# Two FNO attention layers on one core: ones written by GpSimd and VectorE, loads by halves on two queues, the identity loaded first, and another order of the instructions

## The chip, the core and the metric

The kernel runs on one core of one Trainium2 chip. The metric is the device time of one execution in microseconds (us). A core has a matrix engine (TensorE, PE in the profile), three engines for elementwise work (VectorE, DVE; ScalarE, ACT; GpSimd, POOL), and SyncE (SP), which here only issues transfers. Transfers between DRAM and the on-chip memory can be issued by SP and by ACT; the profile calls their issuing queues SPq and ACTq. PE writes its results to PSUM, eight banks of 128 partitions x 2 KB; the other data lies in a memory of 128 partitions.

## The reference

Two layers of the same form are applied to x of shape (2, 56, 128, 128): batch, channels, height, width. Cut to what matters:

```python
xn = inorm(xa, g1, b1)                       # each channel by itself, (2*56, 1, 128, 128)
k, q, v = (fno_layer(xn, w, b, sw, sb) for K, Q, V)   # 8 heads each
scores = einsum('baks,bals->bakl', qh, kh) / 128      # channels against channels, per head
out = softmax(scores) @ vh
out = fno_layer(out, Pw, ...)                # heads back to one channel
att = inorm(out + xa, gan, ban)
an = inorm(att, g2, b2)
h = fno_layer(an, M0w, ..., norm=True, act=True)      # exact gelu
h = fno_layer(h, M1w, ..., norm=True)
y = inorm(h, gmo, bmo) + att
```

`fno_layer` is a spectral convolution (a 2-D real FFT of which 32 x 16 modes are kept, a complex product per mode, and the inverse) plus a 1x1 skip. All arithmetic is fp32.

## The kernel before, in words

The image of one batch lies in `X2` as 128 partitions: channels 0 to 55 at partitions 0 to 55 with one half of the rows (`c`=0), the same channels at partitions 64 to 119 with the other half (`c`=1). Partitions 56 to 63 and 120 to 127 hold ones; one of them serves as a bias row in later matmuls. A load of x (line 328) brings one half of 16 rows of `X2`: 56 partitions x 2 x 4 KB, 448 KB. Sixteen of them bring both batches.

A layer and batch go through these stages; the names are those of the functions:

- `turned` (L496): PE transposes eight rows of the image (16 transposes per unit), ACT or VectorE copies them out of PSUM into `P`, and statistics are taken (VectorE's bn_stats for layer 0, batch 0, otherwise ACT).
- `modes_chain` (L583): mean and variance become the scale `gv` (GpSimd, a power of -0.5, `root`, L313) and the shift `sh`. PE makes the modes of the image from `P`, then four pieces of `P` of 128x1792 are normalised in place (`affine`, L655, on ACT or VectorE).
- `gram` and `gram_chain` (L662, L675): channel-by-channel products over the normalised image.
- `scores`, `values`, `softmax_chain`, `mix_chain`, `heads`, `norms_chain` (L726 to L917): attention in mode space.
- `gelu` (L943): per eight rows the image is formed again (x or the stored result of layer 0 is loaded into one of the three buffers of `xr`, L953), gelu, transposes, and modes.
- `h_chain` and `end` (L1006, L1088): the last spectral part, and per eight rows the result, which goes to `store` (layer 0) or `out` (layer 1). Each is moved in two halves of 224 KB.

`prepare` (L357) makes the layer's weight tables: first 17 small operations on `sm` (GpSimd), then three products over `stage` (the loaded weights, L405 to L407), many small operations, and the tables `WU`, `WT`, `WM`.

Nothing is scheduled automatically. Every operation is recorded as a unit with the engines that could do it (`Work`, L183), and the string `ORDER` (L21) lists all 1410 units in the order of issue, each as the difference to the unit before and a letter for the engine: T for PE, V (and W, a second form) for VectorE, S for ACT, G for GpSimd, Q for SP, N for leaving an optional unit out. `PLACES` (L77) gives the PSUM bank of each result. An engine issues its units in this order and waits, at each, for the data and buffers that the unit needs; a transfer's issue waits in the same way. Since every instruction is issued by one helper, the profile gives L214 as the line of nearly all.

A PE operation uses a tile of the array, by the rows and columns of its weights rounded up to 32, 64 or 128. Two neighbours in PE's order can have different tile shapes; counted over the whole order before, 292 neighbours do.

The first units in the order before, by engine (a half of 16 rows is named by batch, its first eighth of the image g, and c):

- SP: x b0 g4 c0; constants of 416 columns (208 KB, the identity among them); x b0 g6 c0; sm; x b0 g2 c0; x b0 g0 c0; weights (544 KB); constants of 112 columns; then x of batch 1 (seven halves); constants of 768 and 708 columns; the ones (four transfers of 256 KB, two of them before the first loads of xr).
- ACT: x b0 g4 c1, g6 c1, g2 c1, g0 c1; the first copies; x b1 g2 c1.
- GpSimd: clears of xf and xr; the 17 small operations of `prepare`; the three products on `stage`; gv.

Of the kernel before, what the change touches and what calls it, by code (L numbers as in the profile page):

```python
# [14 lines left out]
B, K, N = 2, 56, 128  # L15
# [6 lines left out]
29G -1G -23Q 1S -6Q 52T 1V -46Q 4Q 43V -27G -19S -4S -1Q 82G -83S -1Q 48T 1S 1V -41Q -1Q 7S 39T 1S 32G -31V 32G  # L22
-31T 1V -13T 1S 13V -12V -5T 1S 1V -5T 1S 1V 48G -53T 1S 1V 87V 1T 1V 1G -114Q 55T 21V 40V -39V -57V -3V 35T 76T
-6T 3T -2V 8T -7T 2V 1T -71S 59V -62S -49Q -6Q 131V -124Q 49S 65V 2G 17S -6V -15T 1S 21V -72T 1S 1S -70Q 79T
-29T 22V 73T -59V 60T 1T -100T 36V -35S 3S 80T 3T -52V -24S 34T 56T -13V -132Q 77V -76Q 4Q 129S -56V -22T 1S 2T
1S 21T -32S 35G 54V 8T 1T -57V 49V 9T 2S -68V 10V -31S 32V -47S 103T -53T 55S -93S 94S -90T 1S 72S -44V -4V 7T
-90Q 81V 85T -162Q 145T -67V -22S -50V 74V 12V 18V 53V -31T -133Q 355Q -267V 140V -216V 157T 60T 1V 1G -225V -4Q
158G 2G 4T 1V -19V -1V -55V 284Q 1Q -280G 37S 15G 16T 68S 6T -3G -68T 72V -150V 1V 8G 149T -16V -62S 72T 1V
-145G 74T 62T -61V 68T -4G -141G 149T -95T 94T 11S 106Q -1Q -125S -247Q 173G -67T 260Q -203V -152Q 127V 45T 90T
-87T 1T 560G -548V 51V -52G -91S 151V -90G 1G 99S 478G -472T 1T 1T -76S -125G 194S -247V 239V -2T -65T 68T 1V  # L30
-99G 113T -7S 8T -77V 1T 77T 1T 3S -12T 1V -77V 69G -94G 111S -16S -62S -13T 1V -3T 8T 1V 104T -280G 168S 113S
-190V 187V -3V -183V 91T 62S -74T 13S 1T 1V 75S 2T -75T 77V 1G -94S 17T 1T 1T -4T 77S -72V 1V 100T -95V -4T 100S
-11T -87S 9V 79V -87T 104T -31G -71T 1V 102S -31G -65T 1V -6G 8V 5V 68T -74G 78T 1S -2T 4T 1S -88V 1T 1S -9V 15V
1T 1V 1V 134Q -52T 1S -29T 21T -20V -51T 1V 73T -76T 1V -72G 133G 450G -374T -61T 12V -7T 1S 50T -43S 44V 1N
-71G 20T 73Q -18S 2T -50V -161G 216S -215G 154V 69T 1V -67G 419G -415T 1S 49S 16Q -15S -86G 1G 101T -60T 1T 60V
-12T 1V 13T -61T 66S -73T 8T 61S 1S -69V 3T 42G -44T 1V 6S 1V -43G 83T -36T 1V 60T 5Q 339G -459G -119G 210S 5T
20S -23S 26Q 2T 1V -20N 22Q -17N 16N 18Q -90T 46V -41T 1V 1G 8V -14S 1S 73T -1Q 2S 1G -17T 1S -50V 84Q -6Q 2T 1V
-14T 1S -67T 1V 70S -17T 14S 16T -29V -59G 1T 5G 2V 1T 68T -131G 132S 8Q 3V 2T 1S -2N -88V 74S -3T 20S -83V 385V
-321V 22S -83T 2T 213Q -214V 65T 15T 1S -79V 69N 126Q -199G 194Q 6Q -4T 19Q -129T 109Q 2V 4T -158S 159V 1N -116S
-2S 3T 1V 115T -6N 23Q -222V 206S 4S 1S 7T -149V 22T 2S 130T -4V -127S 2T 2S 125Q 3V -127V 140Q 153G -290V -2V  # L40
287G -173T 1S 178G -296S 131T 1S -19T 184G -167N -16S -110T 2T 1V 1T 1V 127S -11N 22Q -13T -15T 16S 2S -127G 1V
1V 1G 1V 130T 4Q 1T 1S -7Q 2V 1N 22Q -48V -103T 1S 35S 98G -97G -39T 1V 136T 1S 1S -16T 1V -117T 1V 275T 1V 1V
-218S 83T -93N 68T 17S -16V 160V -138Q -4T 5Q 138V -132T -1Q -3S -6S -141G 6S 58V -57G 129T 1V 15S -151T 1V 52N
18N 70T 1V -99S 110T 1S -112T 12V -10G 1W -21N 134S -2T 1S 3T 1S -138T 12W 127T 1V -138N 30G -51T 22V 46N 20S
-65G -13N 141S -148W 8N 1V 42T 106T 2V -120N 13S 79S -77T 52S 52S 2T -107S 99S -86V -9W 106V -1S 2V 4V -139N 13T
1S 233T 1S -267G 22T 1S 133V -122S -43N 160V -94G -63T 66T 95T 2T 2T 1V 2V -1G 2V -115N 13S 211T -277S 278V 3V
-112G 1V 109V -223T 1S 118V -167T 21S -20S 162T 1V 102G -101T 1V 45N 61V -213S 171N -57N -46V 112N -229T 1S 39S
170S 1G -89G 38T 1V -3T 1V 23N 82T 1V -273S -9S 19S 217T 60V -88S 11N 28N 50T 1V 1G -61N 1V 65G -87T 12W 11G 61S
6T 3T -10V 13T -5V 1T 2V 1T -92V 96T -2V -114N -2T -17N 67V -59S 113T -72N 93S -6V -2T 3T -15V 21S -115G 1W 119T
-128V 82T -62G -187Q 285V 3S -79T 87T -140G 54S 1S 86T -107T -13N 3T -12V 119V 4V -76V 83T 1T -40V -296Q 47Q  # L50
181S -10S -209Q -1Q 38Q 190T 1S 103S -11V -147T 113G -110V -167Q 39Q 237G -19G 62T 1T 1T -301Q 156W 95V -103G 9N
-176Q 196Q 40T -36S 10S 113V -1S 232Q -338Q 21S 32V 35G -36V -30S 86T 1V 1V 1G -130Q 28Q 46V -82T 155T 1V -155S
82T -93T 12S -11S 182T -21T 1V -172T 193V -192S 367Q -180T 1V -16T -171S 365Q -279G 70T 19T 9T -10T 2V -302Q
-37Q 281G -243Q 172S 54V -92S 158G 67V 1T -78V -40G 119V -68G -81G 91T 59G 2S 3V -63V -2T -38T 27G -358Q 255Q
182T 1V -410Q 412T 1V -69T 1T -41V 98V -45V -328Q 151Q 176G 2S 1V -93G 83S 62T 3T 111Q -118V 8T 1V -198Q 52V 76T
1S 71T 7V -218Q 317Q -355Q 191T -8T 65T 14T 1T -71S 43T 4V -55S 9T 1S 56V 8S -60T 1T 1T 1T 58V -62T 60V -6T 13T
1T 1T -30V 16V 2V 1V 12T -108V 43S 1V 1T 2S 64S -2T 22T -85V -10T 65T 9T 3S -76V 12V 63V -56V 96T -8T -87T -9T
2T -54V 136S 18T -48S 43S -94V 7V -6G 1G 6G 1V 54T 2V -1S 36S -17T 19S -7T -81G -4V 74V -302Q 18Q 266G 30V -85T
-8T 83T -9G -65V -8V 9V 69T 3T -18T 1V 19V 2T 1S -47V -99G -1G 72T 1V 63G -1G 10T 3T 1T 12V -323Q 236T 1V -72G
2G 218Q -61S -8T 55T -5T -49S 5V 3V 1T 1S 45V 15T -20V 1N -40T 46T 5S -46T -164G 165T -295Q 290V -319Q 56Q 309S  # L60
6T -343Q 344S 8Q 1Q -3V -11T 1V -43T 57T 1V -57T 1S -5T 63T -100G 78N 21N 12Q -76T 66S -58V 5V 57S -11N -6T 44Q
-16Q -80V 53V -218G 173T 2S 9V -56G 46S 67Q 1T 1V -7T -60T 17V -15T 1V 1G 5T 1V 61T -1Q 2V -61G -60G 135Q -18N
-120G 113S 26T -32S 4S -3T 1S -52V 69T 18T -17S 4S -73T 1S 81V 2Q -78V 1V 76N -55S 39N 18Q 2V 1N 47Q -6Q -121T
1V 1V 79T -18T 19S 60Q -94T 38S -37V 13S 2V -60T 1V -73G 190Q -55T 56T -117T 1V 61S 1T 1V 54S -191G 195T -3G
-42S 43Q 3S -45T 31V -30S 3T 43T 1S 4S -47V 1T 1V -67S 42S 21S 47T 1V 8Q -208G 214T -2Q -14S 11T -52T 1S 55Q 2V
1N -21G 15V 7T -6N 11S 6Q -10S -16S -43V 44T 1V 46Q -21Q -409G 340T 4V -2S 1V -2V 5V -165G 229T 5T -67V 65Q 1Q
2S -71T 66V 1N -12T -15T 16S -2S -52T 2T 37V -36V 2V 66T 1S 4S -19T 1V 24Q 2T 1V -81G 2V 1G 80Q 2T -1Q 2S -31T
19T -1S -17V 19V 13T 5S -89V 66T 1V -64T 1S 79G -82T 1V 89T -19T 20V -7S -37S 39T 1S -78V -4T 67V 60S 34S -74T
1V 40G -126T -1V 83S -4S 9T 1S 1V 1T -89V 149T 3T -99G 39V 3V -39S 37V 82S -84S 6V 63N -1G 2N 1W 1N -13N 14Q
-74S 26S 49S -71T 23G 50S -71T 2T 17T -16V 2V 32S -7N -26G 2V 16N -15G 16N 1W 31N 2T 1S -50V 3T -2T 22N 1W 27N  # L70
1Q 10T 11N -48N 28Q -26Q 45G -68S 93N -17N 59N -25S -112V 15N 9Q 48N 1W -11G 1N -47Q 12G 46N 2S 27S -28Q -40N
29N 1W 55S -103S 49N 1Q 1Q -65G 1T 1V 3S 18T 3N 109N -108N 1W 82G -81N 1Q 3N -2S 45N -73T 1V 30T 1N 1V 1N 1Q 1S
69T 3N 1N 1W -30N 31N 2Q 2G 1N 1N 1W 5S -42N 38N 1Q -8Q -24T 3T -1N 9N -1G 2N 1W 1N 2S -12N 1V 1N 1Q -138N 165T
-26Q 29N 8N 1N 1V -11G 2N -23Q 33G -9W 1N 2Q 8Q -67T 11T 1T 1S 1N 36Q -47N 55Q -43Q -11N 12Q -11V 1V 2S -1Q 59Q
# [3 lines left out]
    "6420204640424044362634026671077217004436310467510475230462661303507612242044744205030010240260262041"  # L78
    "6444026244066645644260606244004462662007424610204062624022440106040203440402262206546756523427705440"
    "0052236265326125565365056170100726316002447524250410622526406460022446424264625444206443206660464620"  # L80
    "2070642233644620064004406262"
# [88 lines left out]
N_SMALL = sum(n for _, n in _COLS.values())  # L170
# [63 lines left out]
def fno_layers(ctx: ExitStack, tc: tile.TileContext, x, out, weights, small, const):  # L234
# [82 lines left out]
    def load_const(n):  # L317
        a, b = C_CUTS[n : n + 2]
        move("Q", Ct[:, a:b], const["all"][:, a:b])
# [885 lines left out]
```

## Time and profile before

| | |
|---|---|
| median of three runs | 402.31 us (401.0 to 407.11) |
| the profiled execution | 402.99 us |
| its span, first to last instruction | 401.2 us |
| instructions | 16,362 |
| bytes read, written | 25.34 MB, 14.68 MB |
| mean granted clock of PE | 0.934 |

The page of the profile gives, in this order: busy time per engine; the span in 40 slices; the transfer queues; the chain of work that ended last; the costliest groups of instructions; and the transfers. A row of a timeline has start, length, engine, line, operation, output<-input, shapes and count, and in brackets the idle time before it with what ended it ("issue" when the profile shows no reason). A row of the waits has who waited for whom, the sum in us, the number of waits and the longest.

### The profile page before, as it was taken

The page shows a single profiled execution, that of the slowest core. Times are in us where ns is not written, and L with a number is a line of the kernel's source. Part 1 is how long each engine was busy: PE and PEld are TensorE (multiplying, and loading weights), DVE is VectorE, ACT ScalarE, POOL GpSimd, SP SyncE. Part 2 cuts the span into 40 slices and gives each one's busy share as a digit, 9 for nine tenths or more (in the row PEclk, how much of TensorE's full clock was granted, in tenths as well). Part 3 has the DMA queues.
Part 4 walks back from the last instruction along what each step waited for, and adds up shares of the span by engine and source line. Part 5 has one row for each costly group of instructions (what it writes and reads, how often), then busy time and mean ns, then how long its engine had stood idle before and what let it go on. Part 6 is the DMA issues. An engine that isn't in the chain of part 4 may idle for free.

```text
span 401.2 us, 16362 instructions
## 1 busy us (share of the span) xinstructions
PE 344.8 (86%) x7362; PEld 248.9 (62%) x7362; DVE 279.2 (70%) x513; ACT 223.0 (56%) x338; POOL 223.3 (56%) x222
## 2 busy tenths in 40 slices
PE   1468859999999989998879989999999998998790
PEld 1345748688758556657866976498767555565440
DVE  0688444349794697887788945647876984989990
ACT  1244642353447777998793854432255887797310
POOL 2341002957999985366369393200993875158970
PEclk9999675999999999999768997999999998999997
DMA  7999930130002754322600677000024455201876
GB/s 221 257 214 217 121 74 3 53 60 3 3 4 64 167 141 105 76 54 68 168 2 2 190 229 230 3 5 3 4 69 103 112 132 137 57 2 49 245 255 189
DMA packets 16069, 41.07 MB, mean 102 GB/s; under 512 B 2560, under 2 KB 2688, under 8 KB 16000
## 3 DMA queue, kind: packets, MB, share of 16 engines
q1 hardware_dynamic: 14880, 36.13, 35.3%
q10 hardware_dynamic: 1120, 3.90, 3.2%
q8 instruction: 58, 0.95, 1.0%
q14 instruction: 11, 0.09, 0.1%
HBM read 25.34 MB, written 14.68 MB: 100 GB/s over the span
## 4 chain that ended last, share of the span: by engine, by line
PE 51%; DVE 21%; DMA 13%; issue 6%; ACT 5%; POOL 2%; SPq 0%; DVEq 0%; POOLq 0%; ACTq 0%
PE psum L214 51%; DMA X<-x 9%; DVE P L214 7%; DMA xr<-store 4%; DVE X L214 3%; DVE WU L214 3%; ACT P L214 3%; DVE WT L214 2%; DVE psum L214 2%; DVE WM L214 1%; DVE f L214 1%; ACT WT L214 1%; DVE stage L214 1%; POOL X L214 1%; POOL P L214 1%
## 5 line engine op out<-in xcount | busy, mean ns | idle before, releaser
L214 POOL TENSOR_TENSOR X<-X,gvr 128x1024 f32<-128x1024 f32 x29 | 68.5, 2384 | 2.4 <-issue 2.4
L214 PE MATMUL psum<-P 128*56 128x56 f32 (+2 forms) x1664 | 58.9, 226 | 5.0 <-issue 4.8
L214 PEld LDWEIGHTS psum<-P 128*56 128x56 f32 (+1 forms) x1664 | 51.5, 136 | 11.1 <-issue 7.1
L214 ACT ACTIVATE junk<-P 128x1024 uint8<-128x1024 f32 (+1 forms) x56 | 56.6, 1011 | 0.8
L214 ACT COPY P<-psum 128x1024 f32<-128x1024 f32 (+4 forms) x35 | 27.1, 784 | 52.3 <-PE psum L214 51.1
L214 PEld LDWEIGHTS psum<-C,P 56*128 56x128 f32 (+4 forms) x1124 | 40.9, 159 | 23.3 <-ACT P L214 6.1
L214 PE MATMUL psum<-C,P 56*128 56x56 f32 (+4 forms) x1124 | 49.1, 253 | 4.9 <-DVE X L214 3.3
L214 POOL TENSOR_TENSOR P<-P,X 128x1024 f32<-128x1024 f32 x17 | 39.9, 2361 | 12.1 <-ACT P L214 10.5
L214 PE MATMUL psum<-C,X 56*128 56x56 f32 x512 | 29.0, 281 | 18.8 <-DMA C<-const_all 8.4
L214 ACT ACTIVATE P<-psum,cols 128x1024 f32<-128x1024 f32 x32 | 34.4, 1112 | 12.3 <-PE psum L214 11.7
L214 PEld LDWEIGHTS psum<-C,X 56*128 56x128 f32 x512 | 25.4, 188 | 21.1 <-issue 15.6
L214 DVE COPY P<-psum 128x896 f32<-128x896 f32 (+4 forms) x23 | 21.9, 963 | 23.5 <-PE psum L214 22.4
L214 ACT ACTIVATE P<-psum 128x896 f32<-128x896 f32 (+1 forms) x28 | 24.0, 861 | 23.9 <-PE psum L214 21.4
L214 DVE SCALAR_TENSOR_TENSOR X<-psum,cols,xr 128x1024 f32<-128x1024 f32 x23 | 29.2, 1281 | 10.2 <-PE psum L214 5.7
L214 PE MATMUL psum<-X,BTx 57*64 57x512 f32 x256 | 35.0, 621 | 0.5 <-POOL X L214 0.4
L214 DVE STREAM_TRANSPOSE P<-psum 128x448 f32<-128x448 f32 (+1 forms) x24 | 24.2, 1017 | 4.1 <-PE psum L214 3.6
L214 PE MATMUL psum<-C,WT 32*128 32x128 f32 (+1 forms) x544 | 22.0, 286 | 3.4 <-DVE WT L214 2.0
L214 ACT ACTIVATE P<-P,hs 128x1024 f32<-128x1024 f32 x17 | 19.2, 1145 | 8.7 <-DVE P L214 8.6
L214 POOL TENSOR_TENSOR rs<-k,mhalf 56x2 f32<-56x2 f32 (+1 forms) x8 | 4.9, 621 | 34.2 <-DVE k L214 34.2
L214 PE MATMUL psum<-xf,WU 64*64 64x56 f32 x1024 | 22.3, 242 | 1.7 <-issue 1.7
L214 PEld LDWEIGHTS psum<-C,WT 32*128 32x128 f32 (+1 forms) x544 | 18.9, 189 | 7.8 <-issue 3.4
L214 PEld LDWEIGHTS psum<-xf,WU 64*64 64x64 f32 x1024 | 19.8, 154 | 4.1 <-issue 3.0
(213 smaller groups left out, 669.9 us busy)
## 6 DMA issues: line engine op xcount, KB each, us to landing
xr<-x SPq DMA_DIRECT2D x32, 224.0 KB
store<-X SPq DMA_DIRECT2D x32, 224.0 KB
xr<-store SPq DMA_DIRECT2D x32, 224.0 KB
out<-P SPq DMA_DIRECT2D x25, 224.0 KB
X<-x SPq DMA_DIRECT2D x11, 448.0 KB
X<-x ACTq DMA_DIRECT2D x5, 448.0 KB
out<-P ACTq DMA_DIRECT2D x7, 224.0 KB
stage<-weights SPq DMA_DIRECT2D x2, 544.0 KB
```

Source lines behind the costliest of these rows:

```text
L214: getattr(engines[letter], method)(*args, **kw)
```

## The change

In words:

- A separate first piece of the constants: the identity (128 columns, 64 KB). The other 288 columns of the old first piece are now the second.
- Before each load of 16 rows of x, except the first of batch 0, the whole 128-partition piece (2048 columns) is set to 1.0 by VectorE or GpSimd; the two loads then overwrite partitions 0 to 55 and 64 to 119. These are seven writes: three on VectorE, four on GpSimd. For the piece without one (b0 g4) two transfers of ones remain, of 8 partitions x 8 KB (64 KB each); the four of 256 KB are gone.
- All the loads, and the transfers of xr, store and out, may go to SP or ACT ("QS"); the order says which. Of x, SP gets 9 halves and ACT 7 (before 11 and 5); of batch 1, ACT gets three of eight. In mid-kernel ACT gets four loads of xr from the store, one of xr from x and one transfer to the store; of the output 8 halves (before 7). One of the sm loads and three of the constant pieces move to ACT.
- `ORDER` and `PLACES` are replaced: 1416 units, the same work but for a few choices. PE has 4 matmuls more. Of the four 128x1792 passes of `affine` for batch 0 of layer 0, ACT now does three and VectorE one (before VectorE three); over the kernel ACT does 14 and VectorE 2 (before 8 and 8). GpSimd's elementwise passes of 1024 columns over X2 and P go from 61 to 65. Changes of PE's tile shape between neighbours go from 292 to 233.

The first units in the new order:

- ACT: x b0 g4 c1; identity; x b0 g6 c1, g2 c1, g0 c1; constants of 112 and 288 columns; three copies out of PSUM; x b1 g2 c1; x b1 g0 c0; a copy; another; x b1 g6 c0.
- SP: x b0 g4 c0, g6 c0; sm; x b0 g2 c0, g0 c0; weights; x b1 g2 c0, g0 c1, g6 c1, g4 c1; xr; x b1 g4 c0; ones.
- GpSimd: writes for b0 g6, b1 g6, b1 g2; clear of xr; write for b1 g4; the 17 small operations; two of the products on `stage`, a clear, the third; gv.
- VectorE: the write for b0 g2, a small clear, the writes for b0 g0 and b1 g0, then the first copy.

The diff, with the two strings cut to their first lines:

```diff
 ORDER = """
-29G -1G -23Q 1S -6Q 52T 1V -46Q 4Q 43V -27G -19S -4S -1Q 82G -83S -1Q 48T 1S 1V -41Q -1Q 7S 39T 1S 32G -31V 32G
...
+2S 4V 3G -9S 1Q 57T -48Q 5Q -8Q 30V -34V 17V -9S -3S -3S 54V 1V -47S -1S 14G 29T 1S -15V 20T 3T -7V -5T 10S 3S
...
-C_CUTS = [0, _PARTS["raw"][0], _PARTS["dup"][0], _PARTS["gh1"][0], N_CONST]
+C_CUTS = [0, N, _PARTS["raw"][0], _PARTS["dup"][0], _PARTS["gh1"][0], N_CONST]
...
     def load_const(n):
         a, b = C_CUTS[n : n + 2]
-        move("Q", Ct[:, a:b], const["all"][:, a:b])
+        move("QS", Ct[:, a:b], const["all"][:, a:b])
...
         def load_x(b):
-            for g in range(0, 8, 2):
+            for g in (4, 0, 2, 6):
+                whole = X2[:, b, 8 * g : 8 * g + 16, :].rearrange("p h w -> p (h w)")
+                if b or g != 4:
+                    clear("VG", whole, 1.0)
                 for c in range(2):
                     move(
-                        ("Q", "QS")[c], X2[64 * c : 64 * c + K, b, 8 * g : 8 * g + 16, :].rearrange("p (g r) w -> p g (r w)", r=8),
+                        "QS", X2[64 * c : 64 * c + K, b, 8 * g : 8 * g + 16, :].rearrange("p (g r) w -> p g (r w)", r=8),
                         xin[c, b, :, g : g + 2, :],
                     )

         load_const(0)
         load_x(0)
-        load_const(1)
-        move("Q", stage[:, :1088], weights[0].rearrange("p m r n t -> p (m r n t)"))
+        for n in (1, 2):
+            load_const(n)
+        move("QS", stage[:, :1088], weights[0].rearrange("p m r n t -> p (m r n t)"))
         for n in range(2):
-            move("Q", smt[n], small[n : n + 1, :].to_broadcast([N, N_SMALL]))
+            move("QS", smt[n], small[n : n + 1, :].to_broadcast([N, N_SMALL]))
         load_x(1)
-        load_const(2)
-        load_const(3)
-        for b in range(B):
-            for c in range(2):
-                move(
-                    "Q", X2[64 * c + K : 64 * c + 64, b].rearrange("p (g r) w -> p g (r w)", r=8),
-                    _bc(const["ones"].to_broadcast([8, 1024]), 1, 8),
-                )
+        for n in (3, 4):
+            load_const(n)
+        for c in range(2):
+            move(
+                "QS", X2[64 * c + K : 64 * c + 64, 0, 32:48, :].rearrange("p (g r) w -> p g (r w)", r=8),
+                _bc(const["ones"].to_broadcast([8, 1024]), 1, 2),
+            )
...
-                moved(L, xr[:, n % 3], n, b, None, raw, False, "QQ")
+                moved(L, xr[:, n % 3], n, b, None, raw, False, ("Q", "QS"))
...
-                moved(L, dst, n, b, store if L == 0 else out, None, True, ("Q", "QS" if L else "Q"))
+                moved(L, dst, n, b, store if L == 0 else out, None, True, ("Q", "QS"))
```

More of the change, by code (lines that the diff above doesn't have):

```diff
@@ L27 @@
[L27 to L36, printed above, removed]
@@ L72 @@
[L72 to L74 removed]
+2S 4V 3G -9S 1Q 57T -48Q 5Q -8Q 30V -34V 17V -9S -3S -3S 54V 1V -47S -1S 14G 29T 1S -15V 20T 3T -7V -5T 10S 3S
+-42G 2S 38V -42S 17V 28V -32G 19S 1V -37G 23V 2V 7T 1S -23S -23Q 29G 58G -40V -37Q 80G -70Q 22T 1S 1V -5T 1S 1V
@@ new lines @@
+14T -99G 86S -249S 374Q -358Q 254S -84T 83S -18G -69T 3T -11G 80V 114Q -170T 1S 74T 1S -197V 110V 1T 67T 3T 5V
+-3V -91G -57G 55G 108T -85T -26T 1V 24T 87T -15T 11S -1S 474G -554V 10V -9T 85T -13T -71V 553V -633G 89S 64G -1V
+18S -5T 1T 1T 1T 1T -79V -3G 4T 33V -43T 11S 62S 36T -19V 1V -89T 1V -2S 91T -75T 1T 1T 75V -174G 61G 1G 30T 1V
+7T -4T -44G 138V -11G 23T -148G 5G 144S -102V 85G -84V 5V -4T -9T 1V 59S -49S 82G -12G 460G -462S 19T 1S 11T
+-28T 29S -101V 10V -8T 2T 1V 82T -81G 1G 4T 62V 21T -82V 1G 78T 1S -78V 1V 1T 90T -89V 1V 72T 3T -71T 73S -87T
@@ L75 @@
+2Q -25T 3T 8N 53W -31S 9Q -18Q 41N 1Q 1S -63N 52V 1N 2S -47N 46Q -45W 1N -9V 1N 2Q -1Q 8Q 1S
 """
 PLACES = [int(c) for c in (
[L78 to L81, printed above, removed]
+    "6420204664422264754156061102340274600602040706462633630436557321677220400466766647610101204040002241"
+    "6222646447460445502246206420246202602405262240606526640646002324424602602002464250103112557642700340"
+    "1466402036350543365012756144640746020520244647606076265264102224464540264624452332002424066662026640"
+    "4074620011062642462424420660"
```

84 lines of the change are left out of this document (45 added, 39 removed).

## The prediction

> **What bounds the kernel now.** I read the page's busy line and its chain by engine, then the chain in order of time, then the windows.
>
> ```profile
> PE 344.8 (86%) x7362; PEld 248.9 (62%) x7362; DVE 279.2 (70%) x513; ACT 223.0 (56%) x338; POOL 223.3 (56%) x222
> PE 51%; DVE 21%; DMA 13%; issue 6%; ACT 5%; POOL 2%; SPq 0%; DVEq 0%; POOLq 0%; ACTq 0%
> ```
>
> TensorE (PE) is busy 86% of the span and holds 51% of the chain, with another 6% called "issue". The share is a mean over three stages. Each row below gives a stretch, its length, the busy time of PE, PE's weight loads, VectorE (DVE), ACT and GpSimd (POOL) with their instructions, then PE's granted clock, the DMA share and GB/s:
>
> ```profile
> 0.00:41.40 41.40, 20.27 (x349) 15.76 (x349) 22.91 (x67) 13.44 (x19) 12.51 (x35) 1.00 0.89 224
> 41.40:366.00 324.60, 303.69 (x6716) 220.59 (x6716) 232.76 (x414) 200.50 (x309) 189.19 (x176) 0.93 0.30 75
> 366.00:401.20 35.20, 20.85 (x301) 12.53 (x300) 23.54 (x33) 9.00 (x10) 21.57 (x12) 0.93 0.68 210
> ```
>
> To 41.4 us the DMA engines are the full resource (share 0.89) and PE is idle for 21.1 us. From there to 366 PE is the limit (303.7 of 324.6 us). In the last 35.2 us the output flows at 210 GB/s. The chain in order of time (start, length, what) shows how the first stage ends:
>
> ```profile
> 0.74 5.59 DMA X<-x
> 6.34 14.04 DMA X<-x
> 20.39 14.97 DMA X<-x
> 35.41 3.32 PE psum L214 x111
> 38.73 2.65 issue
> 41.39 11.11 PE psum L214 x250
> 52.49 4.82 issue
> 57.31 29.32 PE psum L214 x669
> ```
>
> Loads of x set the end until 35.4 us. Then PE stands twice, for 2.65 and 4.82 us, with "issue" as reason: nothing that the profile shows released it.
>
> **The first stage: loads.** These windows compare who issues:
>
> ```profile
> 4.00:20.00 16.00, 5.87 (x96) 5.41 (x96) 6.72 (x11) 4.16 (x5) 3.37 (x17) 1.00 0.93 264
> 24.00:36.00 12.00, 9.69 (x123) 5.96 (x123) 9.56 (x36) 5.94 (x11) 3.06 (x4) 1.00 0.93 198
> 41.40:53.00 11.60, 11.09 (x255) 10.18 (x255) 7.66 (x13) 8.17 (x18) 0.00 (x0) 0.72 0.83 108
> ```
>
> ```profile
> 10.38 0.32 ACTq L214 DMA_DIRECT2D X<-x  x1
> 13.05 9.47 SPq L214 DMA_DIRECT2D X<-x  x7
> 27.10 3.74 SPq L214 DMA_DIRECT2D X<-const_ones  x2
> 35.38 0.27 SPq L214 DMA_DIRECT2D X<-const_ones  x1
> 37.69 6.78 SPq L214 DMA_DIRECT2D xr<-x  x4
> ```
>
> ACT issues its last load at 10.38; all later ones come from SP. With both queues filled 264 GB/s moved, with SP's alone 198, at the same share 0.93. From 41.4 to 53, with ones and xr in flight, it was 108 GB/s at share 0.83: the same engines' time for less than half the bytes. The change gives ACT three of the eight second-batch halves (SP keeps five) and cuts the ones from four transfers of 256 KB to two of 64 KB. 198 x 12 is 2.38 MB; at 264 it takes 9.0 us, so 3.0 us is to be had there.
>
> The Trainium skill, "DMA: Bandwidth & Descriptors", section "Issuing engines are not separate DMA queues", speaks against this: all queues run on the same 16 engines, and issuing from several saves only issue time. By it this term is zero, which is rival B below; the 264 and 198 of this trace disagree with it so far, though the transfers' mix differs between the windows.
>
> A later link caps the gain. The first batch's scale (gv) is a GpSimd operation:
>
> ```profile
> 0.82 2.66 POOL L214 MEMSET xr<- 128x3072 f32 x1
> 22.14 2.62 POOL L214 TENSOR_TENSOR stage<-stage,C 128x544 f32<-128x544 f32 x2 [4.19 <-DMA C<-const_all]
> 24.84 1.33 POOL L214 TENSOR_TENSOR stage<-stage 128x544 f32<-128x544 f32 x1
> 27.21 0.73 POOL L214 TENSOR_TENSOR gv<-var,mhalf 128x1 f32<-128x1 f32 x1 [1.04 <-DVE var L214]
> 9.52 1.09 DVE L214 COPY P<-psum 128x896 f32<-128x896 f32 x1 [9.52 <-PE psum L214]
> ```
>
> In the new order gv again stands behind the three products on stage, which need the weights: 2.62 + 1.33 + 0.73 = 4.7 us after these land. The weights are SP's sixth transfer where they were its seventh, so I expect them at about the old 22.1 and gv near 27, against 27.94 (27.21 + 0.73). **Term 1: -2 us**, between the 1 us of this link and the 3 of the transfers; bounds 0 and -3.
>
> The seven large writes of ones cost nothing on the path: a GpSimd memset of 2048 columns is two thirds of 2.66, 1.8 us, and four make 7.1 us:
>
> ```profile
> POOL der L214 <- DMA sm<-small: 10.6, 1, 10.6
> L214 DVE TENSOR_SCALAR P<-P,gv,shz 128x1792 f32<-128x1792 f32 x8 | 9.5, 1198 | 0.0
> L214 ACT ACTIVATE P<-P,shz,gv 128x1792 f32<-128x1792 f32 x8 | 14.8, 1879 | 12.2 <-PE psum L214 9.7 <-DVE shz L214 2.5
> ```
>
> They fit into the 10.6 us in which GpSimd waits for its first input (sm). A VectorE memset of this size isn't in the trace; by the row above it would take 1.2/1792 x 2048 = 1.4 us, by the 896-column copy 2.5; three of them fit into the 9.5 us before VectorE's first operation. Each write stands before a load; the first (1.4 to 2.5 us) is covered by the two loads and the identity already in flight, which land only at 6.3. If that cover failed, it would cost up to 2.5 us. The identity alone (64 KB for 208) lets PE start with the first loads (6.3), worth nothing by itself, as the next loads end later.
>
> ACT now issues seven loads ahead of its first copy and three among the copies. An issue can wait for an earlier load to land:
>
> ```profile
> 0.73 6.23 ACTq L214 DMA_DIRECT2D X<-x  x4
> SPq L214 <- DMA X<-x: 28.1, 13, 3.4
> ```
>
> Four issues held ACT for 6.23 us, until the first loads had landed; seven should end at about the same time, since the later ones wait for the same landings, and the first copy isn't due before PE has done its second unit. Of the three later ones each may wait SP's mean of 28.1/13 = 2.2 us, with copies behind it; PE then waits for loads anyway. I count 0; uncovered, 2.2.
>
> **The two stalls.** PE waits 7.5 us while the other engines are idle and transfers alone run. In the second, ones and xr are what is in flight. With seven eighths of the ones gone, the 1.25 MB of 41.4 to 53 (108 x 11.6) would take 4.7 us at 264. I count the 4.82 as gone, and half of the 2.65, which lies at the tail of the x loads. What is late next is PE itself. **Term 2: -6.1 us**; bounds 0 (the stalls belong to PE's own instruction stream) and -7.5.
>
> The new order gives ACT three of the first batch's four 128x1792 passes (before: VectorE three), and two follow each other before the gram: 2 x (1.88 - 1.20). **Term 3: +1.4 us**; bounds 0 and +2. Over the kernel GpSimd gets four more 1024-column operations:
>
> ```profile
> L214 POOL TENSOR_TENSOR X<-X,gvr 128x1024 f32<-128x1024 f32 x29 | 68.5, 2384 | 2.4 <-issue 2.4
> ```
>
> That is 9.5 us, and 7.1 of writes, on 223.3 busy; it still has 160 idle us. VectorE loses six of the 1.2 us passes and gains about as much in copies and writes. I count both as hidden; uncovered, one 2.38 us operation would show.
>
> **The changes of tile shape.** Counted in PE's program order by rows and columns of the weight tile (32, 64 or 128), the order goes from 292 changes to 233, 59 fewer; the work is four matmuls more. What one costs:
>
> ```profile
> 65.83 0.59 PE L214 MATMUL psum<-mv,C 128*128 128x2 f32 x2
> 66.34 1.98 PE L214 MATMUL psum<-xf,WU 64*64 64x56 f32 x64
> 70.11 0.60 PE L214 MATMUL psum<-P,xf 128*64 128x224 f32 x4
> 70.54 0.55 PE L214 MATMUL psum<-P 128*64 128x224 f32 x4
> 71.02 1.33 PE L214 MATMUL psum<-P,fwg 128*32 128x448 f32 x12
> ```
>
> Four 224-column matmuls take 0.43 us to the next start without a change (70.11 to 70.54) and 0.48 with one: 0.05. Two 2-column matmuls between changes take 0.51 (65.83 to 66.34), where 64 of 64x64 run at 0.03 each: (0.51 - 0.06)/2 = 0.22. I take 0.10, nearer to the first row, since most neighbours of a change are groups of its size. 59 x 0.10 x 0.57 (the chain's share of PE and issue) = 3.4. **Term 4: -3.4 us**; bounds -1.7 and -7.4.
>
> The Trainium skill, "TensorE: Matmul & The Clock Gate", section "Single matmul latency", puts the part of an isolated matmul that doesn't overlap at about 175 ns. As an estimate by that page, a change that exposes all of it would make the term -5.9; the 0.05 row shows less.
>
> **The rest of the order.** I find no chain that it shortens or lengthens for certain, and give 0, with 5 us to both sides, one wait for xr on the chain:
>
> ```profile
> 328.73 5.07 DMA xr<-store
> ```
>
> The end stays: 7.34 MB of output (32 transfers of 0.229) leave in the last 35.2 us; the new order has as many, one more on ACT. 0, bounds -3 and +3.
>
> **Sum.** -2 - 6.1 + 1.4 - 3.4 = -10.1. The profiled execution took 402.99 us (span 401.2), 0.17% above the median of 402.31: 402.99 - 10.1 = 392.9, called 393.
>
> **The rivals.**
> - B: transfers don't get faster and the stalls stay; terms 3 and 4 are left: 402.99 + 1.4 - 3.4 = 401. For it: the stalls name no transfer. Against it: 264 against 198.
> - C (slower): ACT is held by its transfers. It issues five loads or stores in mid-kernel that SP issued before, and an engine that must wait to issue holds what is behind it: copies out of PSUM, for which PE waits in turn.
>
> ```profile
> SPq L214 <- DVE X L214: 79.8, 13, 24.7
> ACT P L214 <- PE psum L214: 95.8, 45, 8.3
> ```
>
> SP's waits for x buffers are 79.8/13 = 6.1 us each; five make 30. ACT has 95.8 us of slack waiting for PE, so I let half hide: 393 + 15 = 408. It decides from 9.3 us of uncovered wait on. All 30 would give 423.
> - D (slower): the weights land late. With everything issued ahead of them (11 halves of 0.459 MB, 0.33 of constants, 0.56 their own) at 198 GB/s they land at 30 us, gv at 35: 7 later. With the stalls as they are, 402.99 + 7 + 1.4 - 3.4 = 408. It decides from a gv 1.3 us later than now on, a landing at 24.5.
> - E: all at the good ends: -3 - 7.5 + 1.4 - 7.4 = -16.5, so 386.5.
>
> **How the numbers follow.** Forecast (its own range 388 to 399) 0.46, E 0.18, B 0.12, C 0.16, D 0.08. Two per cent, about what a measurement of this kernel can tell from no change, is 8.05 us: faster means below 394.3, slower above 410.4. Of the forecast 0.27 lies below 394.3, with E 0.45. Above 410.4 lie the part of C with over 17 us uncovered, 0.10, and half of D, 0.04: 0.14. Within: 0.41. The range goes from 384 (E and 2.5 us of the order) to 411: outside it lie 0.06 below and 0.13 above.
>
> **What would show it.** Right: 264 GB/s, not 198, from 20 us to the end of the x loads; gv before 27.9; no PE stall of several us near 38 and 52; PE's stretch of full work starting some 7 us earlier; ACT's waits for PE no smaller than before. Wrong: stalls as long at the same PE instruction count (term 2 falls); the same rate (term 1); copies on ACT starting late behind a transfer (C); the middle stage no shorter after the stalls are taken out (term 4).

## The result, and the profile after

The changed kernel takes 373.27 us (median of four runs, 371.3 to 375.07) against 402.93 us for the kernel before on the same chip: a ratio of 0.928 (95% interval 0.920 to 0.936), so 7.2% faster. The ratio leaves out executions that lie over 1.5% above the fastest of their kernel, here the 407.11 us of the kernel before; the long ones show a lower granted clock of PE. The forecast was 393 us, in a range from 384 to 411. The profiled execution took 372.01 us, its span 370.2 us, 31.0 us less than before.

The page of the changed kernel gives the busy time by engine, the chain by engine and PE's granted clock in 40 slices; the row behind it is the clock of the kernel before:

```profile
PE 327.4 (88%) x7370; PEld 242.2 (65%) x7370; DVE 266.2 (72%) x500; ACT 230.8 (62%) x344; POOL 243.1 (66%) x232
...
PEclk9999858999999999999959999999999999999996
...
PE 70%; DVE 13%; DMA 5%; ACT 4%; POOL 2%; issue 2%; ACTq 0%; DVEq 0%; POOLq 0%
```

```profile
PEclk9999675999999999999768997999999998999997
```

PE now holds 70% of the chain for 51%, "issue" 2% for 6%, DMA 5% for 13%. And PE's clock has fewer low slices, which the forecast had not looked at. (Half clock means, from here on, a stretch for which the trace records a granted clock of 0.5.)

To see where the time went, I cut both traces not at equal times but at equal work: at the start of PE's 800th matmul pass (the startup is over) and of its 7060th (the last output begins). Windows of before, then of after (length, then busy time and instructions of PE, PE's loads, DVE, ACT, POOL, then PEclk, DMA share, GB/s):

```profile
0.00:66.70 66.70, 40.75 (x800) 34.20 (x804) 34.70 (x90) 25.65 (x47) 12.51 (x35) 0.86 0.72 166
66.70:365.78 299.08, 282.99 (x6271) 201.94 (x6264) 220.75 (x392) 188.30 (x281) 188.97 (x176) 0.95 0.29 76
365.78:401.20 35.42, 21.07 (x304) 12.74 (x302) 23.76 (x33) 9.00 (x10) 21.80 (x12) 0.93 0.68 209
```

```profile
0.00:58.04 58.04, 38.32 (x800) 32.81 (x802) 37.50 (x97) 29.91 (x48) 22.99 (x42) 0.91 0.62 175
58.04:334.75 276.71, 265.90 (x6264) 196.08 (x6264) 204.80 (x372) 192.50 (x288) 202.38 (x181) 0.98 0.30 82
334.75:370.20 35.45, 23.21 (x312) 13.26 (x310) 23.89 (x33) 8.40 (x10) 17.68 (x10) 0.92 0.70 209
```

The start gave 8.7 us, the middle 22.4, the end nothing. For the same 6,260 passes PE was busy 17.1 us less in the middle: the gain lies mostly in how long the passes take, not in long idle stretches.

**Where the middle's 22.4 us are.** I took the start times of all matmul passes and grouped them by unit of the order. The time from the last pass of a unit to the first of the next is a boundary. Up to 0.3 us of each counts as its price, the rest as a wait; what is left is time inside units. For passes 800 to 7060, in us:

| kernel | boundaries with a change of tile shape | without | price of all | waits | inside units | sum |
|---|---|---|---|---|---|---|
| before | 240: 52.5 | 97: 12.8 | 65.3 | 24.0 | 209.8 | 299.1 |
| after | 183: 39.0 | 153: 18.8 | 57.8 | 17.9 | 201.0 | 276.7 |
| difference | | | -7.5 | -6.1 | -8.8 | -22.4 |

A boundary with a change costs 52.5/240 = 0.22 us on the mean, one without 12.8/97 = 0.13. The 7.5 us for 57 fewer changes are 0.13 each. The limit of 0.3 us is a choice of mine, so price and wait are names for two parts of the same boundaries.

**The start.** The chain after, its first long pieces (start, length, what):

```profile
2.56 6.30 DMA X<-x
8.88 10.83 DMA stage<-weights
24.27 8.33 PE psum L214 x89
32.60 6.31 ACT P L214 x5
43.49 11.63 PE psum L214 x235
```

Windows of after, and its rows for gv on GpSimd:

```profile
20.00:28.00 8.00, 3.73 (x42) 2.48 (x42) 5.30 (x18) 3.27 (x6) 4.45 (x5) 1.00 0.91 312
28.00:36.00 8.00, 7.90 (x157) 5.65 (x155) 6.34 (x26) 6.92 (x10) 0.00 (x0) 1.00 0.97 198
```

```profile
22.55 1.33 POOL L214 TENSOR_TENSOR stage<-stage 128x544 f32<-128x544 f32 x1
25.61 0.57 POOL L214 TENSOR_TENSOR gv<-var,mhalf 128x1 f32<-128x1 f32 x1 [1.74 <-DVE var L214]
```

With both queues at work 312 GB/s moved, and 198 again once SP alone issued. No run changed the queue of these loads alone, and the mix of transfers differs between the windows, so that the second queue makes the rate is not shown. The weights landed at 19.71 (8.88 + 10.83), gv was ready at 26.18 (25.61 + 0.57), 1.8 us earlier than before, and it waited 1.74 us for the variance, not for the weights.

PE's waits between 36 and 62 us, first of before, then of after (in total, times, longest):

```profile
PE psum L214 <- issue: 7.5, 2, 4.8
```

```profile
PE psum L214 <- issue: 3.0, 1, 3.0
```

One stall of 3.0 us is left, from 40.47 to 43.49. The transfers of just this stretch hold one packet of queue 8, a queue that carries instructions; the last row is the same for the stall of before from 52.49 to 57.31:

```profile
q1 hardware_dynamic: 28, 0.05, 5.1%
q8 instruction: 1, 0.02, 2.4%
```

```profile
q8 instruction: 1, 0.02, 1.3%
```

So PE stands while its next block of instructions is fetched. The places bear this out. Queue 8 brings 58 packets of 16 KB in after, for 14,740 instructions of PE (7,370 passes and as many weight loads): some 127 passes to a packet. The stalls stand ahead of passes 347 and 602 before (counted from 0) and of pass 475 after, 128 and 127 passes apart. The stall left is thus at another block than the two before, not the rest of one of them. In all ten stalls of 1.7 us or more named issue in the traces of before, after, loads_alone, order_alone, before_xr_late and spare_dma, a 16 KB packet lands within the stall, and PE goes on 1.4 to 1.9 us later. The Trainium skill, "Runtime: NRT & Kernel Launch", section "Instruction fetch mechanics", describes such blocks of 16 KiB on a queue of the engine's own and calls the fetch hidden; the 3.0 us here, and the 7.5 before, were not.

### The profile page after: what moved, and what is told of

Same layout as the page of the kernel before. It is cut to its first block, busy times and chain, and to the rows that moved or that the text cites. A ratio compares the mean times of both kernels' runs of the same rounds, so it can differ in the third digit from the quotient of the medians.

```text
span 370.2 us, 16361 instructions
## 1 busy us (share of the span) xinstructions
PE 327.4 (88%) x7370; PEld 242.2 (65%) x7370; DVE 266.2 (72%) x500; ACT 230.8 (62%) x344; POOL 243.1 (66%) x232
## 4 chain that ended last, share of the span: by engine, by line
PE 70%; DVE 13%; DMA 5%; ACT 4%; POOL 2%; issue 2%; ACTq 0%; DVEq 0%; POOLq 0%
PE psum L214 70%; DVE P L214 3%; DVE WT L214 3%; DVE WU L214 3%; DMA stage<-weights 3%; ACT P L214 2%; POOL X L214 2%; DMA X<-x 2%; DVE psum L214 1%; ACT junk L214 1%; DVE X L214 1%; DVE stats L214 1%; DVE f L214 1%; ACT WU L214 1%; POOL gv L214 0%
## 5 line engine op out<-in xcount | busy, mean ns | idle before, releaser
L214 POOL TENSOR_TENSOR X<-X,gvr 128x1024 f32<-128x1024 f32 x32 | 75.2, 2374 | 0.2
L214 ACT COPY P<-psum 128x896 f32<-128x896 f32 (+4 forms) x30 | 23.6, 805 | 30.1 <-PE psum L214 30.0
L214 PE MATMUL psum<-C,X 56*128 56x56 f32 x512 | 26.3, 269 | 12.6 <-DMA X<-x 11.8
L214 POOL TENSOR_TENSOR P<-P,X 128x1024 f32<-128x1024 f32 x13 | 30.5, 2372 | 10.0 <-ACT P L214 10.0
L214 POOL TENSOR_TENSOR X<-X,xr 128x1024 f32<-128x1024 f32 x10 | 23.6, 2364 | 17.1 <-ACT X L214 14.0
L214 PEld LDWEIGHTS psum<-C,X 56*128 56x128 f32 x512 | 23.5, 178 | 16.5 <-DMA X<-x 6.3
L214 DVE COPY P<-psum 128x896 f32<-128x896 f32 (+4 forms) x27 | 24.4, 918 | 10.6 <-PE psum L214 7.7
L214 ACT ACTIVATE P<-P,shz,gv 128x1792 f32<-128x1792 f32 x14 | 25.5, 1876 | 4.5 <-PE psum L214 4.5
L214 POOL TENSOR_TENSOR WT<-tc,C 128x1024 f32<-128x1024 f32 x8 | 15.3, 1912 | 18.1 <-DVE tc L214 13.0
L214 POOL TENSOR_TENSOR X<-P,X 128x1024 f32<-128x1024 f32 x10 | 23.5, 2374 | 3.7 <-DVE P L214 3.7
```

The costliest lines, as they stand in the source:

```text
L214: getattr(engines[letter], method)(*args, **kw)
```

## The experiments

Two theories stood at first. A: the loads shorten only the start, and the order carries the middle. Its rival: a quieter start keeps the clock up and carries most of it. Within A, theory C says that the order's gain is the price of the shape changes; its rival says that it is waits. Where only ORDER (and PLACES) differ, the diff tells in words what moved.

### Loads and order, each alone

```diff
 loads_alone, from the changed kernel
-ORDER of the changed kernel for all units that begin() doesn't record, and its PLACES
+ORDER of the kernel before for them, and its PLACES
 order_alone, from the kernel before
-ORDER of the kernel before for all units that begin() doesn't record, and its PLACES
+ORDER of the changed kernel for them, and its PLACES
```

> The new loads (writes of ones by GpSimd and VectorE, identity first, three more second-batch halves on ACT, two ones transfers of 64 KB) with the OLD order of all other work and its old PSUM places. Theory A (the order carries the gain): only the start gains, about the 7.5 us by which PE's 400th pass came earlier, so 393 to 397 us. Rival (the loads carry it, and a quieter start keeps the clock up later): most of the 30 us, 373 to 382 us.

> The OLD loads (four ones transfers of 256 KB, 416 columns of constants in one piece, second halves of x mostly on SP) with the new order of all other work and its PSUM places. Theory A (the order carries the gain): 373 plus the start's 7.5 us, so 378 to 384 us. Rival (the loads carry it): 393 to 402 us.

Measured: loads_alone 390.06 us, ratio 0.970 (0.962 to 0.979); order_alone 385.22, ratio 0.959 (0.951 to 0.966). The product of the two is 0.930, the whole change 0.928: the parts add. The windows of the middle, first of loads_alone, then of order_alone:

```profile
54.82:352.23 297.41, 281.89 (x6272) 200.73 (x6264) 219.20 (x393) 188.17 (x281) 189.01 (x176) 0.95 0.28 75
```

```profile
69.96:345.44 275.48, 264.06 (x6264) 195.52 (x6263) 204.56 (x372) 191.95 (x287) 202.38 (x181) 0.98 0.30 82
```

The middle takes 297.4 us with the old order and new loads (299.1 before), and 275.5 with the new order and old loads (276.7 after). It belongs to the order, whatever the start was: theory A. The start belongs to the loads: pass 800 comes at 54.8 with the new loads in the old order, at 70.0 with the old loads in the new order. The loads alone gave more than the 7.5 us expected, since one stall of 2.0 us is all that is left there, and only 3.4 us of half clock follow it. order_alone lies 1 us above what theory A allowed: with the old loads its two stalls took 8.5 us, the longer one 6.8, and 17.1 us of half clock followed. The stall that is left in loads_alone:

```profile
PE psum L213 <- issue: 2.0, 1, 2.0
```

### The early loads of xr put off

```diff
 after_xr_late, SP's part of ORDER; before_xr_late the same with five loads
-  four loads of xr, among the last loads of the start (20 to 34 us)
   weights of the second layer (59 us)
+  four loads of xr
```

> The changed kernel with its four early loads of xr (0.9 MB, issued at 20 to 34 us, first used after 100 us) issued behind the second layer's weights instead (59 us). Theory B (PE's stall of 3.02 us at 40.5 us is an instruction fetch that stands behind the loads, whose last bytes land at 41 us): the loads end some 4 us sooner, the fetch comes sooner, the stall shrinks to under 1 us, and the half clock of 10 us that follows it goes too: 366 to 370 us. Rival (the fetch takes its 3 us at that place whatever is in flight): stall stays at 3 us, 372 to 375 us.

> The kernel before with its five early loads of xr (1.1 MB, issued at 33 to 44 us) issued behind the second layer's weights instead. Theory B (a fetch of PE's instructions stands behind the loads): the stall of 4.82 us at 52.5 us goes or shrinks to under 1.5 us, with part of the half clock behind it: 393 to 398 us. Rival (the stall belongs to PE's own instruction stream): stall stays, 401 to 405 us.

Measured: after_xr_late 366.61 us (366.44 to 367.74), ratio 0.913 (0.906 to 0.920), 6.7 us below the changed kernel. It is the fastest version of this study. The stall is gone (PE has no wait named issue between 36 and 62 us), and so is the half clock behind it. In this trace the stretch from 36 to 41 us holds two packets of queue 8:

```profile
q8 instruction: 2, 0.03, 2.7%
```

The first of them starts at 37.43 us, when PE is at pass 376. In after the fetch of that place starts only at 40.85, 0.4 us after PE has run out at pass 475, with transfers in flight up to there (0.92 MB from 36.0 to 40.47).

Half clock can be priced here, since both kernels run the same passes in the same order, 475 to 658. First after, then after_xr_late:

```profile
43.49:54.02 10.53, 10.53 (x183) 9.59 (x186) 6.88 (x15) 3.14 (x8) 2.71 (x3) 0.51 0.01 3
```

```profile
40.47:46.72 6.25, 6.25 (x185) 5.72 (x187) 6.09 (x13) 5.84 (x14) 0.00 (x0) 1.00 0.03 7
```

10.53 us at 0.51 against 6.25 at 1.00: the stall of 3.0 us cost 3.0 + 4.3.

before_xr_late gave nothing: 402.74 us, ratio 1.003 (0.999 to 1.008). Theory B had promised 393 to 398 us. The waits of its profiled execution (406.90 us) show why:

```profile
PE psum L213 <- issue: 9.3, 3, 3.5
```

Two stalls stayed and a third came at 82.5 us, while the five loads of xr were now in flight. This agrees with fetches that stand behind transfers, but to move the transfers only moved the stalls.

### More transfers

```diff
 spare_dma: after_xr_late, and behind its four loads of xr on SP
+    for k in range(4):
+        move("Q", spare[0, :, 32 * k : 32 * k + 32, :], x[0, :, 32 * k : 32 * k + 32, :])
```

> after_xr_late with four more transfers of 0.92 MB each from DRAM to DRAM (a spare copy of half of x that nobody reads) on SP behind its xr loads, at about 62 to 85 us, where it has no stall of TensorE. Theory B (TensorE's instruction fetches stand behind the transfers in flight): one or more stalls of 2 to 5 us named issue between 60 and 90 us, and half clock behind them: 370 to 378 us. Rival (the stalls at 40 to 57 us belong to that place of the instruction stream): none, 366 to 368 us.

Measured: 368.84 us (368.19 to 370.61), 2.2 us above after_xr_late. One new stall came:

```profile
PE psum L213 <- issue: 2.1, 1, 2.1
```

It stands at 70.5 us, ahead of pass 1240 as the third stall of before_xr_late does, where after_xr_late has none. From 66 to 73 us the transfers run at:

```profile
DMA packets 342, 2.11 MB, mean 302 GB/s; under 512 B 53, under 2 KB 53, under 8 KB 236
```

So transfers in flight can stall PE's fetches away from the startup too. Theory B is right in kind and over-sized: it gave one stall of 2.1 us, at the low end of the 2 to 5 it allowed, with no half clock behind it, and 368.84 us lies below its 370 to 378.

### What a pause costs

```diff
 pauses: after_xr_late, three times, ahead of the mode matmuls of a gelu group
+    move("Q", hold("late1", [N, 32]), hT[1][:, 0:32])
+    move("Q", hold("late2", [N, 32]), hold("late1", [N, 32]))
...
+                    T.matmul(
+                        f1[:32, 511:512], lhsT=hold("late2", [N, 32]), rhs=ident[:, 0:1], start=True, stop=True,
+                        skip_group_check=True,
+                    )
```

> after_xr_late (366.6 us) with three places (about 115, 135 and 280 us) at which TensorE must wait for two small transfers one after the other, each issued only when the copy ahead of it is done. Theory D (a pause of some us is followed by 7 to 14 us of half clock, as in the records of before and after): the pauses of about 3 to 4 us each and as much again for the half clock, 15 to 24 us in all, 382 to 390 us, and PEclk shows a dip behind each place. Rival (the dips have another cause): the pauses alone, 9 to 12 us, 376 to 379 us, and no dip.

Measured: 382.78 us (379.45 to 383.65), 16.2 above after_xr_late. The pauses came out uneven: 2.7 and 2.1 us at two of the places, and 6.1 and 2.3 us where SP, held by the small transfers, had issued a load of xr late. The longest (118.46 to 124.52) and what follows it, then the same passes in after_xr_late:

```profile
118.46:124.52 6.06, 0.59 (x8) 0.00 (x0) 1.33 (x3) 0.51 (x1) 0.00 (x0) 0.85 0.50 116
124.53:139.96 15.43, 15.25 (x161) 10.95 (x162) 9.30 (x20) 8.31 (x11) 14.37 (x29) 0.51 0.48 120
```

```profile
116.79:126.40 9.61, 8.97 (x166) 6.47 (x162) 8.52 (x18) 7.21 (x10) 8.92 (x23) 1.00 0.49 124
```

15.4 us at 0.51 for 9.6 at 1.00: the pause of 6 us cost 6 more afterwards. Of the shorter ones only the last was followed by a dip, of 3.4 us. Theory D holds for the long pause. The Trainium skill, "TensorE: Matmul & The Clock Gate", section "Why this matters for your kernels", asks for no idle gap over about 3 us between bursts. The 3.0, 4.8 and 6.1 us here agree, and so do the 2.1 us of spare_dma, which no dip follows. It doesn't cover all: 6.8 us of half clock follow the 2.65 us stall of before, 3.4 the 2.0 us of loads_alone. And in after a dip of 10.2 us begins at 183.5 us, though in the 20 us before it no step from one pass to the next is over 1.0 us. Its cause stays open.

### The price of a change of tile shape

```diff
 tiny_same, tiny_changed: in each turned() and in the transposes of gelu()
+                if i == 3:
+                    extra(p)
 tiny_same
+            q = slice(64 * c, 64 * c + K)
+            T.matmul(
+                p[:, c, 511:512], lhsT=ident[q, :], rhs=ident[q, 64 * c : 64 * c + 1], start=True, stop=True,
+                tile_position=(64 * c, 0), skip_group_check=True,
+            )
 tiny_changed
+            T.matmul(p[:64, c, 511:512], lhsT=ident[:, :64], rhs=ident[:, c : c + 1], start=True, stop=True, skip_group_check=True)
```

> The changed kernel with two one-column matmuls of the neighbours' shape (56 rows, 128 columns of weights) in the middle of each of 64 groups of transposes, written to unused PSUM columns: 256 passes more and no change of tile shape. By the 0.03 us of one of the 64x64 passes in the trace to 0.06: 8 to 15 us more, 381 to 388 us, by both theories.

> The same with the two matmuls of another shape (128 rows, 64 columns): as many passes, 128 changes of tile shape more. Theory C (a change costs 0.13 us of TensorE's time, the difference of the medians at boundaries with and without one, and all of it stands on the path): 128 x 0.13 = 17 us above tiny_same. Rival (a change costs 0.05 as between the groups of four, and only in the 57% of the time in which TensorE is the path): 4 us above it.

Measured: 381.50 us (381.07 to 384.03) and 395.44 us (391.85 to 404.5). The difference, 13.9 us, over 128 changes is 0.11 us for one. That is near theory C's 17 and far from the rival's 4. The traces say the same of the place itself: at full clock the way from the last transpose ahead of the two extra matmuls to the first behind them takes 0.26 us in tiny_same and 0.48 in tiny_changed (medians of the groups), 0.21 us for two changes. Some 0.05 of it lies between the two extra matmuls, where no shape changes: it belongs to the other weights (128x64 for 56x128), so one change costs 0.08 to 0.11 us.

### More and fewer changes in the order itself

```diff
 after_more:   36 pairs of neighbouring units on T swapped, 233 changes -> 288
 after_flat:   36 other pairs swapped, 233 -> 233
 before_fewer: 35 units on T moved up by at most five places, 292 -> 247
 after_best:   after_xr_late with 16 units on T moved up by at most five places, 233 -> 214
```

In after_flat two of the swaps exchange units that add into one PSUM bank (the modes), so those sums are not the reference's; the instructions are the same.

> The changed kernel with 36 swaps of neighbouring groups on TensorE, each of which adds one or two changes of tile shape (233 to 288 in all), only where the group moved ahead had its inputs by the trace. Theory C: 55 x 0.13 = 7 us more, 378 to 383 us. Rival (the changes cost nearly nothing, the order's gain is in its waits): 372 to 376 us, like after_flat.

> The control: the changed kernel with 36 swaps of neighbouring groups on TensorE chosen in the same way, none of which alters the number of changes (233). Theory C: 371 to 376 us. Rival (any disturbance of the order costs): as much above 373 as after_more.

> The kernel before with 35 groups on TensorE moved up by at most five places where the trace shows their inputs ready: 247 changes of tile shape for 292, everything else as it was. Theory C (0.11 to 0.13 us for a change, as tiny_changed and the boundaries show, and up to 0.25 with the waits that went with the 55 changes of after_more): 45 fewer give 5 to 11 us, 391 to 396 us. Rival (the gain lies in the new order's waits, not in the changes): 399 to 402 us.

> after_xr_late with 16 groups on TensorE moved up by at most five places where their inputs were ready: 214 changes of tile shape for 233. Theory C: 19 changes at 0.13 to 0.25 us, 2.5 to 4.8 us less than the 366.6 of after_xr_late: 362 to 364 us. Rival (the remaining changes sit where another wait would take their place): 366 to 368 us.

Measured: after_more 386.97 us (386.22 to 388.17), 4 us above what theory C allowed, after_flat 374.79 (368.36 to 377.5), before_fewer 402.25 with a ratio of 1.002 (0.994 to 1.010), after_best 371.64 (369.34 to 373.7), which is above after_xr_late's 366.61 and outside what either theory allowed. The table of the middle, as above:

| kernel | with change | without | price of all | waits | inside units | sum |
|---|---|---|---|---|---|---|
| after_more | 233: 49.3 | 103: 14.8 | 64.1 | 24.8 | 203.1 | 292.0 |
| after_flat | 183: 39.3 | 153: 18.3 | 57.6 | 19.7 | 201.7 | 279.0 |
| before_fewer | 202: 44.0 | 135: 18.6 | 62.6 | 24.6 | 208.9 | 296.1 |
| after_xr_late | 183: 39.1 | 153: 18.7 | 57.8 | 17.9 | 201.6 | 277.3 |
| after_best | 166: 35.5 | 171: 22.5 | 58.0 | 22.4 | 202.2 | 282.6 |

Fifty changes put into the order cost 6.3 us as price, as theory C says (0.13 each), and 6.9 us of waits besides; the control, as many swaps without a change, cost 1.8 us of waits in its profiled execution (377.50 us) and nothing clear in its time, 374.79 us for the 373.27 of after. But 38 changes taken out by moving units up gave back only 2.7 us of price in before_fewer, and 17 in after_best gave none: a moved unit's boundary costs (18.6 - 12.8)/38 = 0.15 us without a change, and other waits take what is left. So the price is real and the count is not the lever: theory C falls as the account of the whole gain. Why a moved unit's boundary stays dear was not found.

### What else is in the order

```diff
 one_queue:    after_xr_late, six transfers of xr and store: S -> Q
 old_engines:  after_xr_late, 87 units on the engine of the kernel before: 37 S -> V, 27 V -> S, 14 G -> V, 9 V -> G
 old_then_new: ORDER of loads_alone up to PE's pass 3400, then the rest in the order of after
 new_then_old: ORDER of after up to PE's pass 3600, then the rest in the order of loads_alone
```

In old_engines xr is added twice at two of 32 tiles and not at all at one, since there one operation's engine decides what the next does; at the cuts of old_then_new and new_then_old this holds for one tile each.

> after_xr_late (366.6 us) with the six loads and stores in mid-kernel that ACT issues (xr and store) issued by SP at the same places of the order, as before the change. Theory F (the second queue takes away the waits for xr, 15.7 us of which stood on the chain of before): 372 to 382 us. Rival (the new order issues them early enough on either queue): 365 to 369 us.

> after_xr_late with the engine of the kernel before for 87 operations that the new order gives to another of VectorE, ACT and GpSimd (37 back from ACT to VectorE, 27 from VectorE to ACT, 23 between VectorE and GpSimd), each at its place in the order. Theory G (the choice of engines carries a good part of the 22 us): 375 to 388 us. Rival (the sequence carries it): 366 to 372 us; some loss is likely in either case, since sequence and engines were planned together.

> The new loads, the old order up to TensorE's 3400th pass and the new order for all that is left. Theory A2 (each stretch gains by its own order; the second layer's is worth 17 us): loads_alone at pass 3600 (183.7 us) + the 151.9 us that after takes from there to pass 7060 + 37.5 for the end = 373 us. Rival (the order works as a whole, and what one part leaves undone costs in the next): 380 to 392 us.

> The new loads, the new order up to TensorE's 3600th pass and the old order for all that is left. Theory A2: after at pass 3600 (182.9 us) + the 168.5 us of loads_alone to pass 7060 + 37.9 = 389 us. Rival (the first layer's new order is what lets the second run faster): 374 to 382 us.

Measured: one_queue 370.63 us, but spread from 366.39 to 374.7; its profiled run took 366.39, and its middle is that of after_xr_late (277.35):

```profile
52.55:329.10 276.55, 265.34 (x6264) 195.89 (x6263) 204.31 (x372) 191.98 (x287) 202.36 (x181) 0.98 0.32 85
```

So in this execution the second queue is not what took the waits for xr off the chain; the new order issues these loads early enough on either queue. Theory F (372 to 382 us) falls by this trace; the median alone lies between it and its rival (365 to 369) and would leave it open.

old_engines took 412.97 us (410.81 to 415.07), 46 us more than after_xr_late. Its middle has the same sequence and the same 183 changes, and 43.5 us of waits for 17.9; half clock covers 51 us of this middle and 17 of after_xr_late's. PE's longest waits there, then the longest of after:

```profile
PE psum L213 <- DVE P L213: 11.1, 10, 4.2
PE psum L213 <- DVE WT L213: 5.2, 4, 2.0
PE psum L213 <- ACT WT L213: 3.2, 3, 2.0
```

```profile
PE psum L214 <- DVE WU L214: 2.2, 6, 0.5
PE psum L214 <- DVE P L214: 1.5, 2, 1.1
```

A sequence is worth what the engines that feed it make of it. This doesn't split the order's gain, since the old engines in the old sequence wait 24.0 us, not 43.5; it shows that the two can't be had apart.

old_then_new took 385.68 us and new_then_old 393.01, where theory A2 said 373 and 389. The first lies in the range of the rival, that the order works as a whole (380 to 392 us); the second is nearer to A2 than to its rival (374 to 382). From pass 3600 to 7060 they take 154.9 and 172.0 us (after 151.9, loads_alone 168.5): the second layer runs within 3 to 3.5 us of the pace of its own order, as A2 says. What A2 missed is the cut: old_then_new reaches pass 3600 at 193.4 us, 9.7 later than loads_alone.

## Why the prediction was wrong, point by point

- **Term 1, the loads** (-2): gv came 1.8 us earlier. The size was right by luck, the link was not: gv waited for the statistics of x, and the weights' products were done before. The row of before, with its 1.04 us behind var, said the same: there, too, the products had ended first. The rate was 312 GB/s with two queues, then 198 again. ACT's passes on the first batch (**term 3**, +1.4) stand on the chain after (32.60, 6.31 us) and were not measured alone.
- **Term 2, the stalls** (-6.1): 7.5 us of stalls became 3.0, so -4.5, inside its bounds. The cause, fetches behind transfers, is borne out by after_xr_late and spare_dma. But nothing of the two was left over: both places ran through, and a third, 128 passes behind the first, stood. The other engines were not idle in the stalls either: VectorE was busy for 2.55 of the 4.82 us, GpSimd for 1.24 of the 2.65. Left out of the term was the half clock behind a stall: 4.3 us for one of 3.0. All in all the start gave 8.7 us where terms 1 to 3 said 6.7.
- **Term 4, changes of tile shape** (-3.4, bounds -1.7 and -7.4): mis-sized. The count was right, and 0.10 us lies within the 0.08 to 0.13 measured since. The 0.57 for the chain's share should not have been there: the 64 pairs of changes in tiny_changed take 0.21 us each by the trace, 13.7 in all, and 13.9 us showed in the time. By the table it gave 7.5 us, just past the bound; before_fewer and after_best warn that this is a share in the books, which the count of changes alone doesn't buy.
- **The rest of the order** (0, and 5 to both sides): this step failed. It gave 14.9 us (22.4 - 7.5), half of the whole gain: 6.1 of waits over 0.3 us at boundaries and 8.8 inside units. I had looked for a chain that gets shorter and found none; what got shorter were some 340 boundaries by little each and the time at half clock, which no line of the chain names. order_alone and loads_alone show that this belongs to the order; how much of it each trait of the order buys stays open.
- **The clock** was in no step. By the clock records of the two traces, half clock covers 29.0 us of the middle before and 13.7 after. By the 4.3 us in 10.5 measured above, the 15.4 us less would be worth some 6 us, an estimate. Unit by unit, the 301 units that ran at full clock in both kernels take 2.6 us less after, and the 29 that half clock touched in either take 4.9 less. loads_alone and order_alone, which also have the old and the new order, show it more cleanly: 183.6 and 183.4 us for the units at full clock in both, 20.2 and 14.5 for the touched ones. So most of what was gained inside units, though not all, is half clock. What makes the order do that is argued, not shown: fewer pauses. Nor is the clock most of the whole gain: the fastest execution of the kernel before on record, 394.63 us on another chip, had a mean clock of 0.958, the changed kernel's 371.30 us one of 0.960, and still 23 us lie between them.
- **The end** (0): 35.42 and 35.45 us. Right.

Of the rivals, B falls with the stalls and the start, 8.7 us shorter, D with the weights at 19.71. C had its condition, more transfers issued by ACT in mid-kernel, and one_queue, without them, is no faster. E, all at the good ends, came nearest with 386.5 and still missed 13 us, since it, too, had nothing for the order but the price of the changes.

## What to carry to other kernels

Where a whole order is replaced, compare PE's time at equal work (by count of passes), and give the unknown part of a new order a range as wide as the gaps it could close: PE was busy 283 us in 299, but its boundaries and waits held 89 us, and 29 us of the stretch ran at half clock. Price a stall of TensorE with the half clock behind it: here 3.0 us cost 4.3 more, and 6.1 cost 5.8 more. And put off early loads that nobody needs soon: four loads of xr held up a fetch of instructions and cost 6.7 us.

## What was not expected of the hardware

- A change of tile shape between neighbours on PE cost about 0.1 us by itself (13.9 us for 128).
- PE's instruction fetches can be late behind data transfers: stalls of 1.7 to 6.8 us named issue, at places 127 or 128 passes or a multiple of that apart, with one 16 KB packet of the instruction queue landing in each, 1.4 to 1.9 us before PE goes on. One went when transfers were put off (after_xr_late), one came where transfers were added (spare_dma).
- A stall of 3.0 us was followed by 10.5 us at a granted clock of 0.51 (6.25 us of work at 1.00), one of 6.1 by 15.4 us at 0.51; stalls and pauses of 2.0 to 2.7 us by none to 10.2.
